# Expert routing of layer 0: slot marks in halves of a row, running counts by products on TensorE

## The chip, the cores and the metric

The kernel runs on one core of a Trainium2 chip. Its engines are named as the profile names them: PE (TensorE, matrix products; PEld are its weight loads), DVE (VectorE), ACT (ScalarE), POOL (GpSimd) and SP, whose queue issues most DMAs. The metric is the device time of one execution in microseconds (us), taken as the median of several runs; less is better.

## The reference

Input `x` is 8 batches of 512 tokens of 256 numbers, 4096 tokens in all. Six blocks follow each other, each on a layer norm of `x`: the mixture of experts of layer 0, its windowed attention, the same mixture again, then the mixture of layer 1, its attention, and that mixture again. The change lies in the mixture of layer 0, which runs twice:

```python
logits = xf @ gate_w + gate_b                    # 4096 x 64
top_l, top_i = jax.lax.top_k(logits, K)          # K = 3
gates = jax.nn.softmax(top_l, axis=-1)
fe = top_i.reshape(-1)                           # token by token, choice by choice
oh = jax.nn.one_hot(fe, E)                       # E = 64
pos = (jnp.cumsum(oh, axis=0) * oh).sum(-1) - 1  # place in the expert's list
valid = pos < C                                  # C = 128
buf = jnp.zeros((E, C, D)).at[fe, pos].set(xf[tok], mode='drop')
h = gelu(einsum('ecd,edh->ech', buf, w1) + b1)   # H = 1024
y = einsum('ech,ehd->ecd', h, w2) + b2
out = zeros.at[tok].add(y[fe, min(pos, C - 1)] * (fg * valid)[:, None])
```

So every token picks three of 64 experts, and every expert takes the first 128 tokens that pick it, in token order. `pos` is the number of earlier picks of the same expert.

## The kernel before, in words

The kernel is written with tiles and pools; a scheduler orders the instructions of each engine when the program is built, and each engine then works through its own queue in that order. A pool with `bufs=n` has n buffers for each name: an instruction that writes a tile waits until the buffer's earlier reader is done.

`macaron_kernel` runs `f1.route(2, ...)`, `f1.experts`, the attention of layer 0, `f2.route(1)` and `f2.experts`, then layer 1. The number given to `route` is `bufs` of the pool `tp_`, which holds `sits` and `value`.

`route` loops over the 8 batches ("rows" b). A batch is four tiles of 128 tokens (NT = 4). For each batch:

- `xn` is the normalised batch (statistics L175 and L176 on DVE, L185 on ACT). Two SP DMAs store it (L188) and `x` (L189) for the experts. L92 transposes it on PE, L93 copies it out on ACT.
- L196 gives the gate logits `lg` on PE: 128x64, in four tiles and two parts. L201 adds the bias, L206 and L207 find the three best experts, `ef` is their numbers and `g` their shares (L213 to L221).
- L225 makes `hot` on DVE: for each of 4 tiles x 3 choices, 64 numbers with a one at the chosen expert. Its pool has one buffer.
- L232 and L233 add the three choices to `chosen` (4 tiles x 64 experts).
- L236, L238 and L240 keep the running counts on DVE: `before[i]` is the count of picks of each expert in all earlier tiles, by three additions of 128x64, and `count` passes it on to the next batch.
- L242 and L243 on PE give `pp`, the position of each token in each expert's list: `earlier` (ones below the diagonal) times `chosen`, plus `ones` times `before`.
- L246 multiplies `pp` with `hot`, one instruction for each choice, and L248 adds up: `pos`, 12 positions for each partition.
- L253 on DVE makes `sits`: for each of the 12 a row of 128 with a one at the position. L259 and L263 on POOL make `value`: `hot` times the token's number, and `hot` times its share, three instructions of 128x256 each.
- L268 on PE adds 12 products `sits` x `value` of all batches into one accumulated tile, `table`: for each slot and expert the token number and the share. A 32-bit product is two passes in the trace, so a batch has 24.

After the last batch L275, L276 and L279 turn `table` into `slots` and `gates`. The experts' loop then runs over 64 experts: SP loads of `w1` and `w2` (L289 and L291, five buffers each, 1 MB each) and `b2r` (L293), POOL's broadcast of it (L295), POOL's gather of 128 rows by `slots` (L297), transposes (L303), first product (L312), gelu (L316), second product (L319), bias and share (L321, L322), and a gather-add into the result (L323).

Around the first route the attention's constants are prepared (L359 to L487; its products L407 to L457 stand in PE's queue around the last batch's `table`). The second route is mixed with the end of the attention: its first three batches stand in PE's queue ahead of, and between, the attention's last products (L771, L794, L812), which finish `x` of the last batches.

## Time and profile before

| | us |
|---|---|
| median of 3 runs | 3248.82 |
| lowest and highest run | 3236.14, 3258.50 |
| the profiled execution | 3218.18 |
| its span (first to last instruction) | 3216.4 |
| first route, from 0 to the end of its last table | 125.7 |
| second route, from its first `hot` to the end of its last table | 1355.9 to 1467.5 |
| busy: PE, DVE, ACT, POOL | 2784.4, 1593.0, 1641.3, 1658.6 |

The rows quoted below are of three kinds. A timeline row gives the start (us from the span's start), the time that it took, engine, line, operation, tiles (out<-in) and shapes, how many were merged (x12), and in brackets the idle time of the engine before it with what ended it. A row of groups gives line, engine, operation, tiles and shapes and count, then after the bar the busy us and the mean ns of one, and after the second bar the idle time before. A row of windows gives a stretch with its length, the busy us and number of instructions of each engine, the granted clock of TensorE (1 is full speed), the busy share of the DMA engines and GB/s.

### The profile page before, as it was taken

Reading aid. Unit: us, or ns where it says so; the run is one execution under the profiler, and the core shown is the slowest. Engines: PE = TensorE matmul, PEld = TensorE weight load, DVE = VectorE, ACT = ScalarE, POOL = GpSimd, SP = SyncE. Lnnn points to the kernel's source line nnn. Section 1 sums busy time; section 2 is a strip of 40 time slices with the busy share of each in tenths; the row PEclk is TensorE's granted clock in tenths of the full one; section 3 lists DMA queues with packets and bytes.
Section 4 is the critical chain, followed back from the end, with each engine's and each line's share of the span. In section 5 each row is a group of like instructions: output and inputs, shape, how many; then the busy total and the mean of one; then the engine's idle time right before and its main releaser. Section 6 shows DMA issues by size and latency. Waiting matters only on the chain. (4 is left out here: it accounts for less than half of the span.)

```text
span 3216.4 us, 53865 instructions
## 1 busy us (share of the span) xinstructions
PE 2784.4 (87%) x20353; PEld 1997.6 (62%) x20353; DVE 1593.0 (50%) x3773; ACT 1641.3 (51%) x2608; POOL 1658.6 (52%) x1298
## 2 busy tenths in 40 slices
PE   6699999978888888778999997787899999998783
PEld 6688888833334343467888896575455555554662
DVE  7511111167777777672111113675657666573564
ACT  4133333369999999632333333266444535434452
POOL 3344444368888888524444442255535454324565
PEclk9799999988999999788999997799889989898897
DMA  7599999531555666786999994144101010001355
GB/s 232 192 304 306 306 302 307 171 104 10 78 85 85 84 85 88 84 240 215 307 308 304 303 307 132 40 141 130 29 15 41 28 35 27 20 7 58 109 172 162
DMA packets 378178, 478.66 MB, mean 149 GB/s; under 512 B 93080, under 2 KB 339872, under 8 KB 361536
## 3 DMA queue, kind: packets, MB, share of 16 engines
q1 hardware_dynamic: 339376, 403.50, 44.3%
q0 software_dynamic: 38544, 71.73, 9.5%
q8 instruction: 161, 2.64, 0.3%
q14 instruction: 97, 0.79, 0.1%
HBM read 382.21 MB, written 88.47 MB: 146 GB/s over the span
## 5 line engine op out<-in xcount | busy, mean ns | idle before, releaser
L316 ACT ACTIVATE hT<-hp,b1T 128x128 f32<-128x128 f32 x1024 | 376.0, 368 | 612.7 <-PE hp L312 580.2
L312 PE MATMUL hp<-xeT,w 128*128 128x128 f32 x4096 | 561.8, 280 | 23.6 <-DVE xeT L305 22.5
L312 PEld LDWEIGHTS hp<-xeT,w 128*128 128x128 f32 x4096 | 527.9, 193 | 68.8 <-DVE xeT L305 30.2
L676 POOL TENSOR_TENSOR ud<-dk,dq 128x2048 f32<-128x2048 f32 x128 | 533.4, 4195 | 58.3 <-PE do L692 33.8
L319 PE MATMUL yp<-w,hT 128*128 128x256 f32 x2048 | 506.6, 380 | 0.0
L321 DVE TENSOR_TENSOR y<-yp,b 128x256 f32<-128x256 f32 x128 | 54.3, 425 | 839.0 <-PE yp L319 538.4
L319 PEld LDWEIGHTS yp<-w,hT 128*128 128x128 f32 x2048 | 360.1, 191 | 32.9
L670 DVE SCALAR_TENSOR_TENSOR ub<-bk,relb,bq 128x512 f32<-128x512 f32 x512 | 345.0, 738 | 6.7 <-PE bo L692 6.1
L1804 ACT ACTIVATE pt<-s 128x1024 f32<-128x1024 f32 (+3 forms) x256 | 180.2, 705 | 295.6 <-PE s L1800 233.8
L681 ACT ACTIVATE ud<-ud 128x2048 f32<-128x2048 f32 x128 | 245.0, 1914 | 24.3 <-POOL ud L676 24.1
L295 POOL PARTITION_BROADCAST b<-b2r x128 | 82.2, 646 | 338.7 <-DVE y L321 318.1
L681 ACT ACTIVATE ub<-ub 128x2048 f32<-128x2048 f32 x128 | 245.7, 1920 | 6.7 <-DVE ub L670 6.6
L1737 POOL TENSOR_SCALAR_AFFINE_SELECT d<-d 128x512 f32<-128x512 f32 x128 | 84.6, 661 | 315.6 <-DVE d L1727 315.0
L297 POOL DMA_INDIRECT xe<-f_xn_d,slots x128 | 128.8, 1006 | 216.4 <-PE xp L303 176.5
L323 POOL DMA_INDIRECT f_acc_d<-y,slots x128 | 205.3, 1604 | 60.6 <-DVE y L322 31.6
L1338 POOL DMA_INDIRECT xe<-f_xn,f_tok x156 | 149.7, 959 | 147.2 <-PE tp L1357 73.2
L1727 DVE TENSOR_TENSOR d<-s,fac 128x320 f32<-128x320 f32 (+1 forms) x256 | 120.2, 470 | 210.5 <-PE s L1715 178.7
L1769 POOL TENSOR_TENSOR d<-d,nm 128x640 f32<-128x640 f32 (+1 forms) x128 | 154.7, 1214 | 65.9 <-DVE nm L1749 65.7
L1788 PE MATMUL s<-qm,kp 32*128 32x384 f32 (+2 forms) x768 | 146.3, 458 | 19.7 <-ACT pt L1804 11.0
L1390 ACT COPY we<-wall 128x768 f32 x156 | 129.6, 832 | 47.7 <-DVE xeT L1360 18.5
L692 PE MATMUL bo<-ub,o_w_bond_out 128*32 128x512 f32 x1024 | 145.1, 638 | 9.5 <-ACT ub L681 9.5
L1710 PE MATMUL s<-kp,qp 32*128 32x160 f32 (+1 forms) x1024 | 145.1, 366 | 4.5 <-DVE mx L1732 2.0
(500 smaller groups left out, 5146.6 us busy)
## 6 DMA issues: line engine op xcount, KB each, us to landing
w<-in_L_ffn_w_dram SPq DMA_DIRECT2D x256, 1024.0 KB
vb<-val_d SPq DMA_DIRECT2D x16, 1024.0 KB
pb<-band_d SPq DMA_DIRECT2D x32, 512.0 KB
f_y<-y SPq DMA_DIRECT2D x117, 128.0 KB
f_xn_d<-xn SPq DMA_DIRECT2D x16, 512.0 KB
f_acc_d<-x SPq DMA_DIRECT2D x16, 512.0 KB
x<-f_acc_d SPq DMA_DIRECT2D x16, 512.0 KB
val_d<-vhalf SPq DMA_DIRECT2D x16, 512.0 KB
```

Of the source, the lines that this page charges most:

```text
L312: nc.tensor.matmul(hp[:, jj, :], lhsT=w1[:, kc, :].rearrange("c (j p) -> c j p", j=NJ0)[:, j, :], rhs=xeT[:, kc, :], start=(kc == 0), stop ...
L316: nc.scalar.activation(hT[:, j, :], hp[:, jj, :], AF.Gelu, bias=b1T[:, j, e : e + 1])
L319: nc.tensor.matmul(yp, lhsT=hT[:, j, :], rhs=w2[:, j, :], start=(j == 0), stop=(j == NJ0 - 1))
L323: nc.gpsimd.indirect_dma_start(out=acc_d[:, :], out_offset=bass.IndirectOffsetOnAxis(ap=slots[:, e : e + 1], axis=0), in_=y, in_offset=Non ...
L670: nc.vector.scalar_tensor_tensor(out=ub[:, j, :], in0=bk[:, d : d + T], scalar=relb[:, d : d + 1], in1=t["bq"], op0=ALU.add, op1=ALU.add,)
L676: nc.gpsimd.tensor_tensor(ud, win, t["dq"].unsqueeze(1).to_broadcast([P, 4, T]), ALU.subtract)
L681: nc.scalar.activation(m, m, AF.Gelu)
L692: nc.tensor.matmul(out[32 * j : 32 * (j + 1), :], lhsT=outw[name][:, k, :], rhs=m[:, j, :], start=(k == 0), stop=(k == 3),)
L1338: nc.gpsimd.indirect_dma_start(out=xe[n], out_offset=None, in_=xn_d[h][:, :], in_offset=bass.IndirectOffsetOnAxis(ap=part_of[h]["tok_i"][: ...
L1769: nc.gpsimd.tensor_tensor(d[:, i, :, lo:], d[:, i, :, lo:], pads["nm"][n % 2][:, i, :, x : x + 1].to_broadcast([P, 4, NEAR - lo]), ALU.add,)
L1788: nc.tensor.matmul(tile_[:, j, P:w_], lhsT=pads["k"][g][r, kb * P : (kb + 1) * P], rhs=grp[n]["qm"][r, (kb + 1) * P :], start=True, stop=True,
L1804: nc.scalar.activation(grp[n]["pt"][:, 2 * pair : 2 * pair + 2, :w_], tile_[:, :, :w_], AF.Exp)
```

## The change

Three things change in `route`.

1. `before` and `count` go. `chosen` gets a fifth tile, `chosen[:, NT]`, with the counts of all earlier batches: zero at first, and for the next batch the sum of all five tiles, by one DVE reduction. `pp` is now five products: `earlier` times `chosen`, then for each tile i of the first three `ones` times `chosen[i]`, repeated over the tiles behind it (192, 128 and 64 columns), and `ones` times the fifth tile, repeated over all four (256 columns).
2. The positions are one product on DVE, with `pp` repeated over the three choices, in place of three.
3. `sits` and `value` are made for two tiles at a time, half a batch: two DVE instructions of 768 in place of one of 1536, 12 POOL instructions of 128 in place of 6 of 256. The 12 products into `table` are the same, six behind each half. The pool that holds both tiles has 4 and 2 buffers of half the size in place of 2 and 1.

The condition for the PSUM pool `ps1` is written with `amid` and picks the same pools as before.

```diff
-            count = sp.tile([P, NE0], F32, name="count")
-            nc.vector.memset(count, 0.0)
+            chosen = sp.tile([P, NT + 1, NE0], F32, name="chosen")
+            nc.vector.memset(chosen[:, NT], 0.0)
...
-                before = sp.tile([P, NT, NE0], F32, name="before")
-                nc.vector.tensor_copy(before[:, 0, :], count)
-                for i in range(1, NT):
-                    nc.vector.tensor_add(before[:, i, :], before[:, i - 1, :], chosen[:, i - 1, :])
-                count = sp.tile([P, NE0], F32, name="count")
-                nc.vector.tensor_add(count, before[:, NT - 1, :], chosen[:, NT - 1, :])
...
-                nc.tensor.matmul(pp, lhsT=earlier, rhs=chosen, start=True, stop=False)
-                nc.tensor.matmul(pp, lhsT=ones, rhs=before, start=False, stop=True)
+                nc.tensor.matmul(pp, lhsT=earlier, rhs=chosen[:, :NT], start=True, stop=False)
+                for i in range(NT - 1):
+                    nc.tensor.matmul(
+                        pp[:, i + 1 :], lhsT=ones, rhs=chosen[:, i : i + 1].to_broadcast([P, NT - 1 - i, NE0]),
+                        start=False, stop=False,
+                    )
+                nc.tensor.matmul(
+                    pp, lhsT=ones, rhs=chosen[:, NT : NT + 1].to_broadcast([P, NT, NE0]), start=False, stop=True
+                )
                 at = rp1.tile(wide, F32, name="at")
-                for k in range(TOPK0):
-                    nc.vector.tensor_tensor(at[:, :, k, :], pp, hot[:, :, k, :], ALU.mult)
+                nc.vector.tensor_tensor(at, pp.unsqueeze(2).to_broadcast(wide), hot, ALU.mult)
...
+                if b < NB - 1:
+                    last, chosen = chosen, sp.tile([P, NT + 1, NE0], F32, name="chosen")
+                    nc.vector.tensor_reduce(
+                        out=chosen[:, NT], in_=last.rearrange("p i e -> p e i"), axis=AX.X, op=ALU.add
+                    )
+                for i0 in range(0, NT, 2):
+                    two = slice(i0, i0 + 2)
+                    n = 2 * TOPK0
+                    sits = tp_.tile([P, n, P], F32, name="sits")
...
+                    value = tp_.tile([P, 2, TOPK0, 2, NE0], F32, name="value")
                     for k in range(TOPK0):
...
-            f1.route(2, lambda: next(a1))
+            f1.route(4, lambda: next(a1))
...
-        f2.route(1)
+        f2.route(2)
```

More of the change, by code (lines that the diff above doesn't have):

```diff
@@ L160, in route @@
             ps = rc.enter_context(tc.tile_pool(name=f"{tag}_rps", bufs=2, space=PSUM))
-            ps1 = ps if bufs > 1 else rc.enter_context(tc.tile_pool(name=f"{tag}_rps1", bufs=1, space=PSUM))
+            ps1 = ps if amid else rc.enter_context(tc.tile_pool(name=f"{tag}_rps1", bufs=1, space=PSUM))
             pst = rc.enter_context(tc.tile_pool(name=f"{tag}_rpst", bufs=1, space=PSUM))
             table = pst.tile([P, 2, NE0], F32, name="table")
-            count = sp.tile([P, NE0], F32, name="count")
-            nc.vector.memset(count, 0.0)
+            chosen = sp.tile([P, NT + 1, NE0], F32, name="chosen")
+            nc.vector.memset(chosen[:, NT], 0.0)
             for b in range(NB):
@@ L230, in route @@
                 )
-                chosen = sp.tile([P, NT, NE0], F32, name="chosen")
-                nc.vector.tensor_tensor(chosen, hot[:, :, 0, :], hot[:, :, 1, :], ALU.add)
-                nc.vector.tensor_tensor(chosen, chosen, hot[:, :, 2, :], ALU.add)
-                before = sp.tile([P, NT, NE0], F32, name="before")
-                nc.vector.tensor_copy(before[:, 0, :], count)
-                for i in range(1, NT):
-                    nc.vector.tensor_add(before[:, i, :], before[:, i - 1, :], chosen[:, i - 1, :])
-                count = sp.tile([P, NE0], F32, name="count")
-                nc.vector.tensor_add(count, before[:, NT - 1, :], chosen[:, NT - 1, :])
-                pp = ps.tile([P, NT, NE0], F32, name="pp")
-                nc.tensor.matmul(pp, lhsT=earlier, rhs=chosen, start=True, stop=False)
-                nc.tensor.matmul(pp, lhsT=ones, rhs=before, start=False, stop=True)
+                nc.vector.tensor_tensor(chosen[:, :NT], hot[:, :, 0, :], hot[:, :, 1, :], ALU.add)
+                nc.vector.tensor_tensor(chosen[:, :NT], chosen[:, :NT], hot[:, :, 2, :], ALU.add)
+                pp = ps.tile([P, NT, NE0], F32, name="pp")
+                nc.tensor.matmul(pp, lhsT=earlier, rhs=chosen[:, :NT], start=True, stop=False)
[7 more added lines that the diff above has]
+                )
                 at = rp1.tile(wide, F32, name="at")
-                for k in range(TOPK0):
-                    nc.vector.tensor_tensor(at[:, :, k, :], pp, hot[:, :, k, :], ALU.mult)
+                nc.vector.tensor_tensor(at, pp.unsqueeze(2).to_broadcast(wide), hot, ALU.mult)
                 pos = sp.tile([P, NT * TOPK0], F32, name="pos")
@@ L250, in route @@
                 )
-                sits = tp_.tile([P, NT * TOPK0, P], F32, name="sits")
-                nc.vector.tensor_tensor(
-                    sits, iota.unsqueeze(1).to_broadcast([P, NT * TOPK0, P]),
-                    pos.unsqueeze(2).to_broadcast([P, NT * TOPK0, P]), ALU.is_equal,
-                )
-                value = tp_.tile([P, NT, TOPK0, 2, NE0], F32, name="value")
-                for k in range(TOPK0):
-                    nc.gpsimd.tensor_tensor(
-                        value[:, :, k, 0, :], hot[:, :, k, :],
-                        token[:, b * NT : (b + 1) * NT].unsqueeze(2).to_broadcast([P, NT, NE0]), ALU.mult,
-                    )
-                    nc.gpsimd.tensor_tensor(
-                        value[:, :, k, 1, :], hot[:, :, k, :], g[:, :, k : k + 1].to_broadcast([P, NT, NE0]), ALU.mult
+                if b < NB - 1:
+                    last, chosen = chosen, sp.tile([P, NT + 1, NE0], F32, name="chosen")
+                    nc.vector.tensor_reduce(
+                        out=chosen[:, NT], in_=last.rearrange("p i e -> p e i"), axis=AX.X, op=ALU.add
+                    )
@@ L265, in route @@
+                for i0 in range(0, NT, 2):
+                    two = slice(i0, i0 + 2)
+                    n = 2 * TOPK0
+                    sits = tp_.tile([P, n, P], F32, name="sits")
+                    nc.vector.tensor_tensor(
+                        sits, iota.unsqueeze(1).to_broadcast([P, n, P]),
+                        pos[:, i0 * TOPK0 : i0 * TOPK0 + n].unsqueeze(2).to_broadcast([P, n, P]), ALU.is_equal,
                     )
-                for i in range(NT):
+                    value = tp_.tile([P, 2, TOPK0, 2, NE0], F32, name="value")
@@ L267, in route @@
                     for k in range(TOPK0):
-                        nc.tensor.matmul(
-                            table, lhsT=sits[:, i * TOPK0 + k, :], rhs=value[:, i, k, :, :],
-                            start=(b == 0 and i == 0 and k == 0),
-                            stop=(b == NB - 1 and i == NT - 1 and k == TOPK0 - 1),
-                        )
+                        nc.gpsimd.tensor_tensor(
+                            value[:, :, k, 0, :], hot[:, two, k, :],
+                            token[:, b * NT + i0 : b * NT + i0 + 2].unsqueeze(2).to_broadcast([P, 2, NE0]), ALU.mult,
+                        )
@@ new lines, in route @@
+                        nc.gpsimd.tensor_tensor(
+                            value[:, :, k, 1, :], hot[:, two, k, :], g[:, two, k : k + 1].to_broadcast([P, 2, NE0]), ALU.mult
+                        )
+                    for i in range(2):
+                        for k in range(TOPK0):
+                            nc.tensor.matmul(
+                                table, lhsT=sits[:, i * TOPK0 + k, :], rhs=value[:, i, k, :, :],
+                                start=(b == 0 and i0 + i == 0 and k == 0),
+                                stop=(b == NB - 1 and i0 + i == NT - 1 and k == TOPK0 - 1),
+                            )
```

## The prediction

> **What bounds the kernel now.** I first read the table of windows (length; busy us and instructions of PE, PE's weight loads, DVE, ACT, POOL; granted clock; DMA share; GB/s), to see whether time won in routing reaches the end.

> ```profile
> 100.00:120.00 20.00, 12.07 (x59) 11.00 (x59) 15.54 (x29) 0.00 (x0) 9.65 (x12) 0.70 0.68 243
> 120.00:130.00 10.00, 5.86 (x30) 5.25 (x31) 4.71 (x22) 0.00 (x0) 0.00 (x0) 0.79 0.00 0
> 130.00:150.00 20.00, 14.37 (x64) 12.37 (x63) 2.55 (x6) 4.11 (x9) 7.55 (x9) 0.59 0.18 49
> ...
> 200.00:300.00 100.00, 97.79 (x648) 89.75 (x647) 14.52 (x39) 37.87 (x103) 41.88 (x39) 1.00 0.97 305
> ```

> In the expert stage PE (97.79 of 100) and DMA (0.97) are both full. Ahead of it, from 120 to 130, DMA moves nothing: five experts' weights have landed and their buffers are full until the first expert runs. So the stage starts when routing ends, and time saved in routing moves everything behind it, one for one. Then the timeline of one turn of the routing loop:

> ```profile
> 109.60 1.75 DVE L253 TENSOR_TENSOR sits<-iota,pos 128x1536 f32<-128x1536 f32 x1
> ...
> 111.49 4.84 PE L268 MATMUL table<-value,sits 128*128 128x128 f32 x24 [4.79 <-DVE sits L253]
> ...
> 116.18 0.60 PE L242 MATMUL pp<-chosen,earlier 128*128 128x256 f32 x2
> 116.61 0.59 PE L243 MATMUL pp<-before,ones 128*128 128x256 f32 x2
> 117.24 1.08 DVE L246 TENSOR_TENSOR at<-pp,hot 128x256 f32<-128x256 f32 x3 [2.11 <-PE pp L243]
> 118.36 0.95 DVE L248 TENSOR_REDUCE pos<-at 128x12 f32<-128x768 f32 x1
> ```

> The reader sees a ring: `sits`, `table`, `pp` of the next row (queued behind `table` on PE), `at`, `pos`, `hot`, the next `sits`. From 98.86 to 109.60 it is 10.74 us: sits 1.75, table with its wait 4.8, pp 1.0, at 1.1, pos 0.9, hot 0.9, and semaphores. PE stands idle 4.79 in it; DVE's running sums lie beside `table`. The first route ends serially:

> ```profile
> 121.26 4.44 PE L268 MATMUL table<-value,sits 128*128 128x128 f32 x24 [1.57 <-DVE pack L411]
> ...
> 125.74 0.29 DVE L275 TENSOR_SCALAR empty<-table,row 128x64 f32<-128x64 f32 x1 [4.54 <-PE table L268]
> ...
> 133.84 1.17 POOL L297 DMA_INDIRECT xe<-f_xn_d,slots  x1 [18.79 <-PE wq L457]
> ```

> The second route (one buffer) has POOL in the ring as well, as its timeline shows:

> ```profile
> 1437.89 0.96 DVE L225 TENSOR_TENSOR hot<-iota,ef 128x768 f32<-128x768 f32 x1 [0.55 <-POOL value L263]
> ...
> 1449.72 1.17 DVE L225 TENSOR_TENSOR hot<-iota,ef 128x768 f32<-128x768 f32 x1 [0.25 <-POOL value L263]
> ...
> 1457.75 0.61 POOL L259 TENSOR_TENSOR value<-hot,token 128x256 f32<-128x256 f32 x1 [7.19 <-PE table L268]
> ...
> 1460.68 2.17 DVE L253 TENSOR_TENSOR sits<-iota,pos 128x1536 f32<-128x1536 f32 x1
> ```

> POOL waits there until the whole table is done, and `hot` and `sits` then wait for POOL. Its first turns stand in PE's queue ahead of the attention's last products (L771 at 1393.36, behind a table begun at 1389.22), so they count too. Prices come from the groups of the first 127 us:

> ```profile
> L253 DVE TENSOR_TENSOR sits<-iota,pos 128x1536 f32<-128x1536 f32 x8 | 14.0, 1752 | 0.0
> ...
> L238 DVE TENSOR_TENSOR before<-before,chosen 128x64 f32<-128x64 f32 x24 | 10.5, 439 | 0.1
> ...
> L225 DVE TENSOR_TENSOR hot<-iota,ef 128x768 f32<-128x768 f32 x8 | 7.5, 942 | 0.0
> ```

> **The change part by part**, for 16 turns (8 batches, two routes).

> *Half of sits.* `table` begins after 768 marks instead of 1536. A DVE product of 768 elements is L225: 0.94; L253 takes 1.75. Saved per turn 0.81. The second half runs beside the first twelve passes of `table` (half of 4.84). 16 x 0.81 = **-13.0**.

> *One product for positions.* Three of 256 take 1.09 from first start to last end. One of 768 lies between 0.94 (L225) and 1.09; PSUM is read now as well, so I take 0.95. 16 x 0.14 = **-2.2**.

> *Five products in place of two.* Each is two passes. At full clock passes of 256 columns start 0.216 apart (four of them 116.18 to 117.20 with the drain), passes of 128 and of 64 0.111 (1.77 for sixteen of L196, with its drain). For 192, between these, 0.163. New: 2 x (0.216 + 0.163 + 0.111 + 0.111 + 0.216) = 1.63; old 4 x 0.216 = 0.86: +0.77 per turn, between +0.67 (192 as cheap as 128) and +1.30 (all as dear as 256). A gain is excluded: three more stand in one in-order queue. 16 x 0.77 = **+12.3**; the two first turns run at half clock (L242 1.19 for a pair at 31.24, 1.22 at 1358.21), where it is twice that: **+1.5**. The repeated right operand has no row: between nothing and twice the four `ones` products, +1.2; I take nothing, as DVE's repeated operands in L225 and L253 cost nothing.

> *Running sums off DVE.* Gone per turn: three L238 at 0.44, count (0.36), copy (0.20): 1.88. New: a sum of five, 256 elements in, between 0.16 (L218, 12 in) and 0.95 (L248, 768); by the line through both 0.41. Beside `table` this is worth nothing. It counts where the ring waited for DVE: L243 0.82 at 82.34 and `at` 1.69 late at 84.73, `at` 1.59 late at 60.75 (pp ended 59.16), L243 0.96 at 1360.63. By at most 1.47 in a turn: 1.47 + 1.47 + 0.96 = **-3.9**.

> *Half of value, two buffers in the second route.* POOL takes 12 of 128 for 6 of 256 (0.61). One is between 0.31 and 0.61; by L1769 (640 elements, 1.21) and L259, 0.41: 4.9 for 3.7 per turn, with room in a ring above 10. In the second route the first half starts when half the table is done; the second takes 2.5 after it, while pp, at and pos take 3.6. So `hot` stops waiting: 0.55, 0.25, 0.22 (1.17 for 0.95) and 0.42 (the 2.17): **-1.4**. At 0.61 each that gain is gone.

> *Order.* Built, the changed program differs only in the two routes. In PE's queue the next rows' transposes and gate products stand otherwise: 20 ahead of table 0, 15 of table 1, 21 of 2, 24 of 4, 8 of 5, where before it was 24, none, 30, 23 of 3, 11 of 4. Sixteen take 3.5 (1425.66 to 1429.20), which PE's idle time covers; the excess cost 1.7 at table 0 (sits done 40.57, table 42.29) and 3.0 at table 2 (65.32, 68.31). I take the same again, +-3. On SP two stores of `xn` in the first route move behind the small loads, directly ahead of the first weights; these landed by 114, the first expert ran at 138.6, so 20 us cover it. On POOL one broadcast (0.46) moves behind the second route's first gathers: **-0.5**.

> Sum: -13.0 - 2.2 + 12.3 + 1.5 - 3.9 - 1.4 - 0.5 = **-7.2 us**: nearly all of what the halves win goes back into the three more products. On the profiled execution, 3218.18 (span 3216.4, 1.8 around it), that is 3211. The median of the runs is 30.6 above that execution: 3248.8 - 7 gives **3242**.

> [...] POOL's first `value` at 99.11 takes 1.97 while L253 runs, 0.61 alone, and L232 beside POOL takes 0.83 for 0.41. [...]

> **Rivals.**
> *DVE bound the first route.* From 40 to 100 it is busy 54.3 of 60 (18.12 + 16.86 + 19.35). If all five turns there shorten by 1.47, not two, and the queue order saves its 3: -4.4 - 3 more, 3234. Against it: `at` waits for pp in most turns.
> *The five products cost more than they free* (slower). Place: between the last pass of `table` and `at`. If the repeated operand is read at half rate, pp takes 1.2 more: +19 - 7 = +12, 3261. It decides once pp passes 2.2 us (1.02 now, plus the 0.95 of sits and at, plus 0.3 of the rest per turn).
> *The clock stays up.* `table` runs at a granted clock of about half (0.58 from 108.0 to 116.1, 1.00 in the 1.2 us of pp). PE's gap falls from 4.79 to 3.85; if that kept it at full, passes go from 0.213 to 0.111, 2 us per turn, -32 more: 3210. [...]
> [...]

> **Chances.** Forecast (-14 to +1) 0.56; DVE 0.16; five products 0.16; clock 0.05; lock 0.07. The range takes in all but the clock, with the runs' own spread (3236 to 3258, 11 to each side): 3217 to 3266. One per cent, 32 us, is about what a measurement of this kernel can tell from no change: faster 0.06 (clock), slower 0.03, within 0.91.

> **What would show it.** The ring in the first route's last turns at 10.3 to 10.7; `table` in two runs of 12 passes, the first 0.95 after `hot`; pp 1.7 to 1.9 long in place of 1.0; `at` in one instruction of 0.95; no wait of `hot` for POOL after 1400; first gathers 3 to 5 us sooner in each route. Wrong if pp passes 2.2 us, if the clock in `table` is not near 0.6, or if the gathers move and the end does not.

## The result, and the profile after

The changed kernel took 3231.9 us (median of 20 runs) where the kernel before, run beside it, took 3251.9 (also 20 runs): a ratio of 0.995, 95% interval 0.9932 to 0.9968, so 10 to 22 us less. A second comparison, in later runs where before took 3293, gave 0.9931 (0.9904 to 0.9959), 14 to 32 us less. The sign of the forecast holds, and 3231.9 lies in its range, 3217 to 3266. Its size, 7 us, lies under both intervals, and the gains, 16 and 23 us by the two ratios, lie beyond the forecast's own band of -14 to +1. The gain is two to three times what was worked out.

The profiled execution of the changed kernel has a span of 3227.7 us, longer than the 3216.4 of before. That says nothing against the gain: the profiled execution of before (3218.2 us in all) was 34 us quicker than the median of its 20 runs. In the two profiles the attention between the routes (first to last `ub` on DVE, 649.2 before, 667.5 after) and everything behind the last product of the second layer-0 mixture (1245.8 before, 1260.3 after) are 33 us longer together, although the order of instructions there is the same but for a few neighbours on PE that changed places. So the profiles are compared only where the change is: from the first `sits` of a route to the last pass of its `table`. I call that the route's stretch. Repeated kernels show how far one profile's stretch can be trusted: the changed kernel's two routes together took 170.6 us in one profile and 172.5 in another, a third kernel's (below) 165.6 and 168.7. Of the kernel before there is one profile only, from the earlier runs.

The table of windows over the two stretches, of the kernel before (its columns are length; busy us and instructions of PE, PE's weight loads, DVE, ACT, POOL; granted clock; DMA share; GB/s):

```profile
38.82:125.70 86.88, 62.42 (x336) 57.71 (x336) 72.25 (x233) 18.14 (x37) 37.01 (x42) 0.76 0.65 222
1364.83:1467.54 102.71, 70.88 (x652) 65.27 (x651) 69.81 (x251) 25.98 (x50) 28.01 (x55) 0.80 0.70 209
```

The same for the changed kernel:

```profile
37.84:113.31 75.47, 57.50 (x378) 52.60 (x378) 63.86 (x199) 21.04 (x40) 42.93 (x84) 0.89 0.78 262
1366.56:1461.72 95.16, 73.56 (x697) 67.74 (x696) 66.87 (x212) 25.96 (x50) 33.70 (x96) 0.86 0.74 219
```

The stretches fell by 11.4 and 7.6, together 19.0 us; the runs show 16 and 23. The reader should look at two columns. PE has 42 instructions more in the first route (378 for 336) and is yet busy 4.9 us less. And the granted clock of PE rose, from 0.76 to 0.89 and from 0.80 to 0.86. (The records of the clock begin at 47.28 us before and at 35.10 after; for earlier times the view shows 1.00.) Nothing in the forecast's sum moves that column.

One turn of the first route after the change, from the timeline (start, length, engine, line, operation, and in brackets the idle time before it and what ended it), which answers to the ring shown of before:

```profile
98.57 2.02 DVE L261 TENSOR_TENSOR sits<-iota,pos 128x768 f32<-128x768 f32 x2
...
99.67 4.54 PE L276 MATMUL table<-value,sits 128*128 128x128 f32 x24 [3.86 <-DVE sits L261]
...
104.05 0.60 PE L236 MATMUL pp<-chosen,earlier 128*128 128x256 f32 x2
...
104.48 0.88 PE L238 MATMUL pp<-chosen,ones 128*128 128x192 f32 x6
...
105.20 0.65 PE L242 MATMUL pp<-chosen,ones 128*128 128x256 f32 x2
105.89 0.96 DVE L246 TENSOR_TENSOR at<-pp,hot 128x768 f32<-128x768 f32 x1 [4.21 <-PE pp L242]
106.88 0.95 DVE L248 TENSOR_REDUCE pos<-at 128x12 f32<-128x768 f32 x1
```

`table` begins 1.10 us behind the start of the first half of `sits`, where it began 1.90 behind the start of the whole: 0.80 won. pp runs from 104.05 to 105.85, 1.80 us, where it was 1.03. `at` is one instruction of 0.96 where three took 1.09. These are the forecast's 0.81, 0.77 and 0.95. What is not in the forecast is the length of `table`: 4.54 here, 2.84 to 2.92 in three of the first route's turns, where before seven of eight took 4.27 to 5.46. The groups of instructions by line, of the first 115 us of the changed kernel (busy us, mean ns):

```profile
L276 PE MATMUL table<-value,sits 128*128 128x128 f32 x192 | 30.8, 333 | 13.3 <-DVE sits L261 13.3
...
L261 DVE TENSOR_TENSOR sits<-iota,pos 128x768 f32<-128x768 f32 x16 | 15.6, 1014 | 0.0
```

Eight `table` take 30.8 us there; they took 37.2 before. In the second route it is 35.0 for 39.0. That is 10.4 us of the 19.0. With it the forecast's sum, -7.2, would have been -17.6.

The first route's end, and the first gather behind it, now come here (133.84 before for the gather):

```profile
108.97 4.34 PE L276 MATMUL table<-value,sits 128*128 128x128 f32 x24 [0.77 <-DVE sits L261]
...
121.55 1.17 POOL L305 DMA_INDIRECT xe<-f_xn_d,slots  x1 [16.75 <-PE wq L465]
```

And in the second route `hot` no longer waits for POOL, while POOL still waits for `table`:

```profile
1446.04 0.95 DVE L225 TENSOR_TENSOR hot<-iota,ef 128x768 f32<-128x768 f32 x1
...
1450.78 0.40 POOL L267 TENSOR_TENSOR value<-hot,token 128x128 f32<-128x128 f32 x1 [5.49 <-PE table L276]
```

```profile
95.07:98.48 3.41, 0.89 (x4) 0.44 (x3) 2.76 (x9) 0.21 (x1) 0.00 (x0) 1.00 1.04 398
98.48:101.90 3.42, 1.15 (x5) 1.18 (x6) 3.42 (x5) 0.00 (x0) 2.79 (x3) 0.50 1.11 376
101.90:105.31 3.41, 3.41 (x18) 3.41 (x17) 2.73 (x8) 0.00 (x0) 2.52 (x4) 0.50 1.01 378
105.31:108.72 3.41, 1.39 (x9) 0.94 (x7) 1.95 (x4) 0.00 (x0) 0.00 (x0) 1.00 1.08 402
```

After, with the gap from 95.80 to 99.67 and `table` from 99.67 to 104.21:

```profile
93.13:96.54 3.41, 2.68 (x19) 2.22 (x18) 2.69 (x13) 0.21 (x1) 1.69 (x5) 1.00 1.00 373
96.54:99.95 3.41, 0.28 (x2) 0.31 (x3) 3.38 (x5) 0.00 (x0) 1.15 (x2) 1.00 1.09 398
99.95:103.37 3.42, 3.42 (x18) 3.42 (x17) 1.69 (x3) 0.00 (x0) 3.42 (x8) 0.50 1.07 360
103.37:106.78 3.41, 2.48 (x18) 2.03 (x16) 0.89 (x1) 0.00 (x0) 1.43 (x4) 1.00 1.02 393
```

The reader should hold the busy us of PE (the first number behind the length) against the granted clock of the slot below (third number from the right). Before, two slots in a row have little work (0.89 and 1.15 of 3.41 us), and two slots follow at half clock, which take in 20 of the 24 passes. After, only one slot is nearly idle (0.28), and only one follows at half clock. A pass starts 0.213 us after the one before at half clock and 0.111 at full. 24 passes take 5.46 where none is at full clock and 2.84 to 2.92 where all are; 4.54 is about 16 slow ones and 8 quick ones.

The same holds over both routes of all twelve profiles (slots that begin at 25 to 125 us and at 1355 to 1485 us). Of slots at full clock, all 117 in which PE was busy less than 45% of the time were followed by half clock, and 372 of the 403 others by full. Of slots at half clock, none of the 77 with PE busy less than 75% was followed by full clock, and 138 of the 158 with 85% or more were. So what a gap costs here goes with its length and with how it lies over the slots. The slots do not keep step with the program: one begins 95.07 us behind the span's start before, and one 93.13 after, 1.94 apart. Two profiles of one kernel with the same order on PE (halves, one `at`, below) have eight `table` of the first route in 31.0 and in 33.5 us.

### The profile page after: what moved, and what is told of

Its sections match the earlier page's. It is cut to its first block, busy times and chain, and to the rows that moved or that the text cites. A ratio compares the mean times of both kernels' runs of the same rounds, so it can differ in the third digit from the quotient of the medians.

```text
span 3227.7 us, 54108 instructions
## 1 busy us (share of the span) xinstructions
PE 2800.5 (87%) x20449; PEld 2006.0 (62%) x20449; DVE 1581.2 (49%) x3691; ACT 1643.2 (51%) x2610; POOL 1672.4 (52%) x1394
## 5 line engine op out<-in xcount | busy, mean ns | idle before, releaser
L684 POOL TENSOR_TENSOR ud<-dk,dq 128x2048 f32<-128x2048 f32 x128 | 533.1, 4194 | 74.2 <-PE do L700 46.0
L329 DVE TENSOR_TENSOR y<-yp,b 128x256 f32<-128x256 f32 x128 | 54.3, 424 | 838.5 <-PE yp L327 550.8
L331 POOL DMA_INDIRECT f_acc_d<-y,slots x128 | 205.3, 1604 | 65.4 <-DVE y L330 31.6
L700 PE MATMUL bo<-ub,o_w_bond_out 128*32 128x512 f32 x1024 | 147.2, 649 | 10.3 <-ACT ub L689 9.6
L700 PE MATMUL do<-ud,o_w_damage_out 128*32 128x512 f32 x1024 | 141.6, 626 | 10.8 <-ACT ud L689 10.8
```

The lines of the kernel that those rows point to most:

```text
L331: nc.gpsimd.indirect_dma_start(out=acc_d[:, :], out_offset=bass.IndirectOffsetOnAxis(ap=slots[:, e : e + 1], axis=0), in_=y, in_offset=Non ...
L684: nc.gpsimd.tensor_tensor(ud, win, t["dq"].unsqueeze(1).to_broadcast([P, 4, T]), ALU.subtract)
L700: nc.tensor.matmul(out[32 * j : 32 * (j + 1), :], lhsT=outw[name][:, k, :], rhs=m[:, j, :], start=(k == 0), stop=(k == 3),)
```

## The experiments

Two theories of the surplus stood against each other at first. **Clock**: the halves of `sits` shorten PE's idle gap ahead of `table` (from 4.8 to 3.9 us in the turns shown), and with that more of its passes run at full clock. **DVE**: it is the running sums that left DVE. A variant of Clock held that not the gap but pp's additional work keeps the clock up. Each kernel's runs are compared with runs of before on the same chip; there before took 3293 to 3295 us (3251.9 in the first comparison of the changed kernel). All numbers are gathered here: ratio to before; the two routes' stretches; the sums of eight `table` in each; and the granted clock of the two stretches.

| kernel | ratio (95%) | stretches, us | `table`, us | clock |
|---|---|---|---|---|
| before | 1 | 86.9 + 102.7 | 37.2 + 39.0 | 0.76, 0.80 |
| changed, first profile | 0.995 (0.9932–0.9968) | 75.5 + 95.2 | 30.8 + 35.0 | 0.89, 0.86 |
| changed, again | 0.9931 (0.9904–0.9959) | 74.9 + 97.6 | 30.4 + 33.8 | 0.86, 0.86 |
| halves alone | 0.9931 (0.9903–0.996) | 74.2 + 96.1 | 33.1 + 34.5 | 0.84, 0.84 |
| without halves | 1.0004 (0.9973–1.0035) | 87.0 + 106.4 | 36.6 + 38.8 | 0.78, 0.82 |
| changed + fillers, route 1 | 0.9928 (0.9902–0.9955) | 70.3 + 94.8 | 24.8 + 31.6 | 0.98, 0.87 |
| changed + old sums | 0.9948 (0.9923–0.9972) | 78.4 + 99.5 | 31.4 + 35.2 | 0.85, 0.83 |
| before + fillers | 0.9967 (0.9939–0.9994) | 76.5 + 98.3 | 24.8 + 30.5 | 0.98, 0.89 |
| halves, one `at` | 0.9906 (0.9874–0.9937) | 72.3 + 93.2 | 31.0 + 31.7 | 0.88, 0.86 |
| the same, again | 0.9891 (0.9861–0.9921) | 74.5 + 94.2 | 33.5 + 31.5 | 0.82, 0.86 |
| the same + fillers | 0.9926 (0.9896–0.9955) | 72.1 + 96.9 | 26.6 + 28.2 | 0.95, 0.90 |
| the same + late fillers | 0.99 (0.987–0.9931) | 71.4 + 97.7 | 29.3 + 29.4 | 0.93, 0.87 |

**The halves alone.** The kernel before, with the loop over halves of the changed one:

```
-                sits = tp_.tile([P, NT * TOPK0, P], F32, name="sits")
+                for i0 in range(0, NT, 2):
+                    two = slice(i0, i0 + 2)
+                    n = 2 * TOPK0
+                    sits = tp_.tile([P, n, P], F32, name="sits")
...
-            f1.route(2, lambda: next(a1))
+            f1.route(4, lambda: next(a1))
...
-        f2.route(1)
+        f2.route(2)
```

> Halves of `sits` and `value` alone, with the buffers that go with them; the running counts stay on DVE, the positions in three products. Result to be explained: the changed kernel gained about 16 us where 7 were forecast, and in its profile the first route ended at 113.3 us where it had ended at 125.7, of which 6.4 is a faster `table` (37.15 us in eight turns before, 30.8 after). Theory Clock: `table` became faster because PE's idle gap ahead of it fell from 4.8 to 3.9 us, so that more of its passes ran at full granted clock. The halves alone cut the gap by 0.8, so `table` should take 31 to 33 us in eight turns here too, and with the two cheap products (1.0 in place of 1.8 per turn) the first route should end at 108 to 111, the time 22 to 27 us under the kernel before. Theory Clock with busy products: not the gap but the longer pp (1.8 us of work) holds the clock; then `table` takes 36 to 37 here, the route ends at 116 to 119, the time is 13 us under before. Theory DVE: the surplus came from the running sums that left DVE; they are still there, so again 119 and 13 us, with `table` starting late behind DVE.

Measured: 22.7 us under before (13 to 32), the first route's stretch 74.2, its end at 108.2, `table` 33.1. Time, end and (within 0.1) `table` are those of theory Clock by the gap. The end owes 4.8 us to a first `sits` that came sooner than before's (34.0 for 38.8), so it is the stretch and `table` that decide. The variant had `table` at 36 to 37, and both it and theory DVE had the first route 7 to 10 us shorter than before (116 to 119 for 125.7); the stretch fell by 12.7. With pp back at 1.03 us, the longer pp can't be what holds the clock. It also says that the halves alone make the whole gain. The table of windows over its two stretches shows the clock:

```profile
34.01:108.21 74.20, 55.62 (x336) 49.42 (x336) 66.56 (x241) 20.93 (x39) 41.71 (x84) 0.84 0.79 265
1363.51:1459.62 96.11, 67.16 (x646) 60.38 (x645) 69.89 (x259) 26.39 (x50) 34.20 (x96) 0.84 0.75 215
```

PE has here exactly the 336 instructions that it had before, and is busy 55.6 us with them instead of 62.4.

**The other part alone**, running counts on TensorE and positions in one product, with whole marks and values (the changed kernel with the loop over halves taken back):

```
-                for i0 in range(0, NT, 2):
-                    two = slice(i0, i0 + 2)
-                    n = 2 * TOPK0
-                    sits = tp_.tile([P, n, P], F32, name="sits")
+                sits = tp_.tile([P, NT * TOPK0, P], F32, name="sits")
```

> Running counts on TensorE and positions in one product alone; `sits` and `value` whole, buffers as before. Theory Clock (by the gap): the gap stays at 4.6 to 4.8 us, `table` takes 36 to 37 us in eight turns as before, the five products cost 6.2 + 0.8 in the first route and `at` and DVE give back 1.1 + 2.9: the first route ends at 127 to 129, the time is 4 to 8 us above before. Theory Clock with busy products: pp's 1.8 us keep the clock up, `table` takes 31 to 33, the first route ends at 122 to 124, the time is 4 us under to 0. Theory DVE: the surplus of 9 us over the forecast belongs to this part, so the first route ends at 120 to 122 and the time is 2 to 5 us under before, with `table` as long as before and `at` starting without a wait for DVE.

Measured: 1.0004 of before, that is 1 us above it (9 under to 12 above); stretches 87.0 and 106.4, 3.8 above before together; `table` 36.6 and 38.8, as before. The first route ended at 122.4, where Clock had it at 127 to 129: its first `sits` came 3.5 us sooner than before's (35.3 for 38.8), in a part of the trace that varies from execution to execution by as much (37.8 and 34.0 in the changed kernel's two profiles), so the stretch decides, not its end. Theory DVE asked for a gain of 2 to 5 us here and a quicker first route; neither is there. Its timeline keeps the old gap and the old price:

```profile
95.22 5.46 PE L272 MATMUL table<-value,sits 128*128 128x128 f32 x24 [4.75 <-DVE sits L257]
```

A gap of 4.75 us, and all 24 passes at half clock, although pp is the long one.

**The changed kernel with fillers in the first route**, products that nobody reads:

```
+FILL = 4
...
+            idle = pst.tile([P, NT, NE0], F32, name="idle") if amid else None
...
+                for _ in range(FILL if amid else 0):
+                    nc.tensor.matmul(idle, lhsT=ones, rhs=chosen[:, :NT], start=True, stop=True)
                 at = rp1.tile(wide, F32, name="at")
```

> The changed kernel with four more products per turn in the first route (256 columns, behind pp, into a PSUM tile that nothing reads): they only keep PE busy for 1.7 us (3.4 at half clock) of its idle 3.9 between pp and `table`. Theory Clock: the idle gap falls to about 2.1 us, `table` runs at full clock in nearly all turns (2.7 to 3.0 us each, 22 to 25 us in eight turns, 30.8 in the changed kernel), the first route ends at 105 to 108 instead of 113.3, and the time is 5 to 8 us under the changed kernel, 20 to 26 under before. Theory DVE, and the products theory of the forecast: `table`'s price has nothing to do with PE's gap; the fillers hide in idle time, the first route ends at 113 to 116 and the time is that of the changed kernel or 1 to 3 us more.

Measured: `table` 24.8 us in eight turns, seven of them at 2.84 to 2.92; the stretch 70.3, 5.2 under the changed kernel's first profile; the end at 108.2. The end had been expected at 105 to 108. Its time, 0.9928 of before (24 us less), can't be told from the changed kernel's 0.9931, so the 5 to 8 us that Clock had promised in time are not shown. The window of the first route:

```profile
37.91:108.19 70.28, 63.16 (x448) 58.38 (x447) 63.16 (x199) 21.45 (x39) 42.61 (x84) 0.98 0.81 274
```

448 instructions on PE where the changed kernel has 378 in its stretch, and it is 5 us shorter, at a granted clock of 0.98.

**The changed kernel with the old running sums on DVE as well**; their result is read by nothing:

```
+                before = sp.tile([P, NT, NE0], F32, name="before")
+                nc.vector.tensor_copy(before[:, 0, :], count)
+                for i in range(1, NT):
+                    nc.vector.tensor_add(before[:, i, :], before[:, i - 1, :], chosen[:, i - 1, :])
+                count = sp.tile([P, NE0], F32, name="count")
+                nc.vector.tensor_add(count, before[:, NT - 1, :], chosen[:, NT - 1, :])
```

> The changed kernel with the old running sums computed on DVE as well (copy, three sums, count, 1.9 us per turn), their result unread. Theory Clock: they lie beside `table`; the first route ends at 113 to 116, the time is 0 to 4 us above the changed kernel (the forecast's -3.9 for three waits is given back at most). Theory DVE: the surplus was theirs; the first route ends at 120 to 124 and the time is 9 to 16 us above the changed kernel, 0 to 7 under before.

Measured: 0.9948 of before, 17 us less (9 to 25), within the changed kernel's own two results. The first route ended at 111.8, but its first `sits` came 4.4 us sooner than in the changed kernel; its stretch is 2.9 us longer than the changed kernel's, where theory DVE asked for 7 to 11. Theory DVE falls as the source of the surplus. Relief of DVE is worth something, though: the two stretches are 5 to 7 us longer than the changed kernel's, and in two turns of the first route PE now stands and waits for `chosen` (1.70 and 1.92), which it did in none:

```profile
100.51 0.67 PE L244 MATMUL pp<-chosen,earlier 128*128 128x256 f32 x2 [1.92 <-DVE chosen L235]
```

This kernel carries the old sums and the new reduction, more than either kernel, so 5 to 7 is an upper bound of what the old sums cost.

**The kernel before with fillers, and nothing of the change.** If the clock is the cause, work that is only added must make that kernel faster:

```
+FILL = 6
...
-            table = pst.tile([P, 2, NE0], F32, name="table")
+            marks = pst.tile([P, 2 + NT, NE0], F32, name="table")
+            table, idle = marks[:, :2], marks[:, 2:]
...
+                for _ in range(FILL if b else 0):
+                    nc.tensor.matmul(idle, lhsT=ones, rhs=before, start=False, stop=False, skip_group_check=True)
                 at = rp1.tile(wide, F32, name="at")
```

> The kernel before, with nothing of the change, and six unread products per turn behind pp in both routes from the second turn on (256 columns, 2.6 us at full clock, 5.2 at half, in an idle gap of 4.8). Theory Clock: the gap falls to about 2.2 us, `table` takes 24 to 28 us in eight turns instead of 37 to 39, the first route's stretch 75 to 79 us instead of 86.9, and the time is 18 to 24 us under before, although only work was added. [...]

Measured: 0.9967 (0.9939 to 0.9994), 11 us under before (2 to 20), although every instruction of before is still there and 84 products more (6 in 7 turns of two routes). `table` fell to 24.8 and 30.5, 20.9 us less; the first stretch is 76.5, as Clock had it, and the second fell by 4.4. The time gained is less than the 18 to 24 us expected. The last three turns show where the rest went (timeline of this kernel):

```profile
96.01 0.70 PE L245 MATMUL pp<-before,ones 128*128 128x256 f32 x2 [1.77 <-DVE before L240]
...
96.55 2.75 PE L247 MATMUL table<-before,ones 128*128 128x256 f32 x12
...
101.17 2.92 PE L272 MATMUL table<-value,sits 128*128 128x128 f32 x24 [1.87 <-DVE g L215]
...
105.33 0.70 PE L245 MATMUL pp<-before,ones 128*128 128x256 f32 x2 [0.81 <-DVE before L240]
```

`table` is done in 2.92, and then pp stands for 0.8 to 1.8 us and waits for the running sums: with the clock at full, DVE is what the ring waits for.

**Halves and one `at`, the running counts left on DVE**, the part of the change that costs PE nothing (edit shown against the halves alone); and the changed kernel itself once more, against the same runs of before:

```
-                for k in range(TOPK0):
-                    nc.vector.tensor_tensor(at[:, :, k, :], pp, hot[:, :, k, :], ALU.mult)
+                nc.vector.tensor_tensor(at, pp.unsqueeze(2).to_broadcast(wide), hot, ALU.mult)
```

> Halves of `sits` and `value` and `at` in one product; running counts on DVE, pp in two products, no fillers. The forecast's prices, with the clock's share taken from the halves alone: 22 us under before for the halves, 2 for `at`, so 24 under before, and 8 to 10 under the changed kernel, whose five products are left out. If the five products cost nothing on the whole (the kernel with them and whole marks took 1.0004 of before), this stands level with the changed kernel, within 4 us.

> The changed kernel itself, on the chip and against the runs of before that the other three share, so that they can be compared with it. By its first comparison (0.995): 10 to 22 us under before. By theory Clock it is 16 to 24 above the kernel with halves and fillers, and 0 to 6 above the kernel before with fillers.

> The same kernel without fillers once more, against the same runs of before: by its first comparison 0.9906 (0.9874 to 0.9937), 20 to 41 us under before; the first route's stretch 70 to 75 us, `table` 29 to 33 us in eight turns of the first route.

Measured: 0.9906 (0.9874 to 0.9937) and, again, 0.9891 (0.9861 to 0.9921), so 31 and 36 us under before, where the prices had given 24; the changed kernel beside the first of them 0.9931 (0.9904 to 0.9959), 23 under. Two expectations for the changed kernel failed: it stands level with halves and fillers (0.9926, below), not 16 to 24 us above, and about 12 us under before with fillers, not above. The medians of halves with one `at` and of the changed kernel differ by 8.6 us (3256.4 and 3265.0), the stretches of the two profiles of each by 4.4 on the mean (167.1 and 171.5). By these figures the five products cost 4 to 9 us more than their relief of DVE gives back, where the forecast's terms say 12.3 + 1.5 - 3.9 = 9.9. The intervals overlap, so that this kernel beats the changed one is likely and not certain. None found is quicker; the one with late fillers, below, is level with it.

**The same with fillers**, four in seven turns of each route; in a second kernel only in the last three turns of each (`b >= 5` in place of `b`):

```
+FILL = 4
...
+                for _ in range(FILL if b else 0):
+                    nc.tensor.matmul(idle, lhsT=ones, rhs=before, start=False, stop=False, skip_group_check=True)
```

> Halves of `sits` and `value`, `at` in one product, running counts left on DVE and pp in its two products; from the second turn on, in both routes, four more products per turn behind pp (256 columns, into free columns of `table`'s PSUM bank, read by nothing). From the first sits to the last pass of `table` the first route took 86.9 us before, 75.5 in the changed kernel, 74.2 with the halves alone, 70.3 in the changed kernel with fillers. Theory Clock: the fillers bring the idle gap from about 4.0 to 2.3 us; `table` takes 23 to 26 us in eight turns of each route (33.1 and 34.5 with the halves alone), the first route's stretch is 64 to 67 us, and the time is 34 to 42 us under the kernel before. If the fillers bring nothing beyond the halves: 72 to 75 us for that stretch, 20 to 25 under before.

> Halves and `at` in one product, counts on DVE (the best so far, 0.9906 of before), with the four unread products per turn only in the last three turns of each route. With them in seven turns PE's queue took another order, in which one turn of each route waited about 6 us for the next row's gate products (16.07 us from sits to sits in one turn, where the others took 9); in this kernel the first route's order on PE is that of the kernel without fillers but for the fillers. Theory Clock: the last three `table` of the first route take 2.9 us each (together 8.8 where the kernel without fillers took 11.75), its stretch from the first sits to the last pass is 68 to 70 us (72.3 without fillers, 72.1 with fillers in seven turns), the second route's 88 to 91 (93.2), the time 4 to 8 us under the kernel without fillers. If that order was not what ate the fillers' gain: 72 and 93 again, the time the same.

Measured: 0.9926 and 0.99, no better than the same kernel without fillers (0.9906, 0.9891). `table` did what was expected: 26.6 and 28.2 with seven turns, and the last three of the first route at 2.92, 2.90 and 2.92 with late fillers. The stretches did not follow: 72.1 and 71.4 in the first route where 64 to 67 and 68 to 70 were expected, and 97.7 in the second with late fillers where 88 to 91 were. In the first of the two, one turn took 16.07 us (its timeline):

```profile
62.06 2.92 PE L275 MATMUL table<-value,sits 128*128 128x128 f32 x24 [0.91 <-DVE sits L260]
...
64.82 1.90 PE L198 MATMUL lg<-gate_w,xnT 128*128 128x64 f32 x16
...
66.75 0.42 DVE L203 TENSOR_TENSOR logits<-lg,gate_b 128x256 f32<-128x256 f32 x1 [0.93 <-PE lg L198]
...
68.93 0.96 DVE L227 TENSOR_TENSOR hot<-iota,ef 128x768 f32<-128x768 f32 x1
...
71.67 0.70 PE L244 MATMUL pp<-chosen,earlier 128*128 128x256 f32 x2 [1.00 <-DVE chosen L235]
```

The fillers had changed the order of PE's queue: the gate products `lg` of the row stood behind the `table` of the row before, where without fillers they stood ahead of it, and so `logits`, `hot` and `chosen` came late and pp began 6.7 us after `table` had ended. The late fillers left the first route's order on PE as it was, but in its last turn pp waited 1.84 us for `chosen`, and in a turn of 14.16 us of the second route, which both kernels have, pp began 5.8 us after `table` had ended, behind late gate products. What one would gain with the clock at full and the order kept is not shown.

## Why the prediction was right, and where its size was wrong

**Time and range.** That the time lies in the range says little: 49 us wide, it took in every rival but one, and the surplus of 9 to 16 us over the forecast fits into it. Of the signs that the forecast named, pp's length, `at`'s length and `hot` without a wait came; the ring did not (10.04 and 9.29 in the first route's last turns, for 10.3 to 10.7), nor did the first gather (12.3 us sooner in the first route, for 3 to 5).

**Half of sits** (-13.0). Right as worked out: `table` starts 0.80 us sooner in nearly every turn. But the step priced what it moved and took the moved instruction at its old length. This is the term that was mis-sized: `table` stood in the ring as "table with its wait 4.8" and was left there. It lost 10.4 us in the two routes, and 8.6 with the halves alone.

**The clock stays up** (rival, 0.05, 3210). It was put as all or nothing: 32 us if the clock stayed at full, nothing otherwise, and its low chance was the author's estimate, with no run behind it. The runs showed something between: behind a shorter gap fewer of the passes are slow. The 192 `table` of the twelve profiles, sorted by the idle time of PE just ahead of them (in the profiles of before and after, no pass of a `table` under 3.2 us starts more than 0.2 us behind the one before; of one of 4.7 or more, 16 to 23 of the 23 do):

| idle ahead, us | count | mean `table`, us | under 3.2 | 3.2 to 4.7 | 4.7 or more |
|---|---|---|---|---|---|
| under 0.5 | 70 | 3.42 | 49 | 13 | 8 |
| 0.5 to 2 | 36 | 3.64 | 20 | 14 | 2 |
| 2 to 3 | 25 | 4.23 | 6 | 15 | 4 |
| 3 to 4.05 | 31 | 4.60 | 2 | 22 | 7 |
| 4.05 to 4.6 | 16 | 4.98 | 0 | 8 | 8 |
| over 4.6 | 14 | 5.00 | 0 | 3 | 11 |

The mean rises with the gap, but the gap straight ahead explains only part of the 10.4. Five of the 16 turns had a gap of 4.46 to 5.50 us before and have one of 3.12 to 3.94 after; there `table` fell by 2.3 us together. The other 8.1 lie in turns where PE's queue put other products ahead of `table` or where it had stood behind no long gap before (the first route's fifth `table` took 5.46 behind 1.40 us, and 2.84 behind none after). How much of that is the change, how much the order that came with it and how much the lie of the slots in these profiles isn't separated. The trace of before had only a weak hint: its one short `table` (2.92, in the fourth turn) stood behind an idle time of 0.59, but four others behind 0.00 to 0.62 took 4.27 to 5.28.

**One product for positions** (-2.2). `at` takes 0.96 for 1.09, as taken. In time it can't be told apart.

**Five products in place of two** (+12.3 and +1.5). pp is 1.80 long for 1.03 in most turns: the 0.77 was exact, so taking a pass of 192 columns between its neighbours, and the repeated operand at nothing, gave the whole. It passes the 2.2 us from which the rival "five products cost more" decided in three turns only: in the two first turns (3.54 and 3.57; passes of 256 columns start 0.53 to 0.59 us apart there, for 0.22 in the turn shown, and over the second of them the granted clock is 0.50), and in one where eight of the attention's passes stand among the five (2.68).

**Running sums off DVE** (-3.9). The waits of pp for the sums went (0.42 at 82.34 and 0.56 at 1360.63 on PE itself), but `at` is still late in two turns of the first route (1.31 and 1.46, for 1.59 and 1.69), which gives back 0.5 of the 2.9 taken there. So the places named show about 1.5 of the 3.9. The old sums, put back beside the new reduction, lengthen the stretches by at most 5 to 7 us. The size is thus open between these. With the sums put back it is pp, which waits for `chosen`, more than `at` that shows them. The rival **DVE bound the first route** (3234) gave nearly the measured time, by the wrong mechanism.

**Half of value, two buffers** (-1.4). `hot` waits for POOL no more, and one of the twelve takes 0.40, for the 0.41 taken.

**Order** (-0.5, PE's queue at +-3). The first `table` starts 1.3 us behind its `sits` where before it was 3.5. Whether the +-3 held as a whole is not shown, since the order also changes the clock of `table`; the fillers' kernels show that an order can be worth 6 us in one turn.

**The sum.** The products' part as a whole was put at +12.3 + 1.5 - 2.2 - 3.9 = +7.7; measured +1 (9 under to 12 above), in the stretches +3.8 (whole marks with the rest of the change, against before). The halves' part was put at about -15; measured -23 (-32 to -13), in the stretches -19.3. So "nearly all of what the halves win goes back into the three more products" was wrong: of the 19 to 23 us that the halves win, 1 to 4 go back by these two kernels, and 4 to 9 by the comparison with halves and one `at`.

**Lock** (0.07). That DVE and POOL lock each other out is not shown by any run. What the traces show is longer instructions side by side: POOL's first `value` beside `sits` took 1.97 at 99.11 before, for 0.61 alone, and 1.87 at 48.28 after, for 0.40. For the ring it did not decide: the first halves of `sits` took 0.94 to 0.96 in all 16 turns and `hot` 0.92 to 0.96. Only second halves were longer, 1.15 in five turns, and `table` does not wait for them.

## What to carry to other kernels

Behind PE's idle gaps in the ring the products had no fixed price here (the 24 passes of `table` took 2.84 to 5.46 us): read the granted clock in and behind the gap, and price an edit that shortens the gap (or lengthens it) with the passes that change clock, not only with the time that it moves. In the twelve profiles half clock followed on all 117 slots of 3.41 us at full clock with PE busy less than 45% of the time, and full clock on 372 of the 403 others. Parts of a change with opposite signs should be run apart: here one half made the whole gain, and the other cost some of it. When a product's wait is taken away, look at what is late next: with the clock at full it was the running sums on DVE, and with an altered queue a row's gate products.

## What the runs showed that was not expected

Work that nothing reads made a kernel faster: six products per turn in idle time, and the kernel before took 0.9967 (0.9939 to 0.9994) of its time, its first route's granted clock rising from 0.76 to 0.98.

Slow passes also stood behind gaps shorter than a slot of 3.41 us, and half clock followed on slots that were not wholly idle: before, PE was busy 0.89 us of the slot at 95.07, and the next was at 0.50. Of 25 `table` behind an idle time of 2 to 3 us, 15 took 3.2 to 4.7 us and 4 took 4.7 or more, where 2.84 to 2.92 is the length with all passes at full clock.

The granted clock fell one slot behind the gap: in the turn shown after the change it was still 1.00 in the slot that the gap filled (96.54 to 99.95, PE busy 0.28 us), and 0.50 in the next (99.95 to 103.37), in which PE worked on the passes of `table` throughout.
